# A selective-scan kernel on one core: GpSimd's work taken as pairs of state groups, and a convolution's taps gathered into one part

## The chip, the core and the metric

The kernel runs on one core of a Trainium2 chip. The core has five engines that run their own instruction streams: TensorE (PE in the profile), VectorE (DVE), ScalarE (ACT), GpSimd (POOL) and SyncE (SP), which here issues nearly all DMAs. Each engine takes its instructions strictly in the order in which they stand in its stream; between engines there are semaphores only. SBUF is the on-chip memory of 128 partitions, PSUM the small memory into which TensorE accumulates. The metric is the device time of one execution in microseconds (us).

## What is computed

The input is a batch of 32 images, 96 channels, 56 x 56. Layer 0 is a ConvNeXt block, layer 1 two Mamba blocks with a fusion and a batch norm. Cut to what matters:

```python
# layer 0
h = depthwise_conv7x7(x) + conv_b
h = layernorm_over_channels(h)
x1 = layer_scale * (gelu(h @ w1 + b1) @ w2 + b2) + x
# layer 1: seq is x1 as (batch, 3136 tokens, 96); two times:
h = layernorm(seq)
xs, z = split(h @ in_w)                       # 192 channels each
xc = silu(causal_conv4(xs) + conv_b)
dt, Bm, Cm = split(xc @ xproj_w)              # 6, 16 and 16 columns
delta = softplus(dt @ dt_w + dt_b)
dA = exp(delta[..., None] * A)                # 192 channels x 16 states
dBx = delta[..., None] * Bm * xc[..., None]
hstates = scan over tokens: h[t] = dA[t] * h[t-1] + dBx[t]
y = sum over states of hstates * Cm + Dp * xc
seq = seq + (y * silu(z)) @ out_w
# then: pooled branch, 1x1 fusion, batch norm over everything, + x1
```

All of it is in 32-bit floats.

## The kernel before, in words

Before the main loop the depthwise convolution of the first 12 images is made on TensorE with banded weight matrices, the weights are folded, and the first image's layer-0 block is made. After the main loop there is a short pass for the batch norm and the output.

**Stages.** The main loop has 256 stages: 32 images x 4 chunks of 784 tokens (`CH`) x 2 Mamba layers. Layers alternate, so a stage's successor is another chunk or the other layer. In a batch's first chunk the scan starts from the constant 0, in the others from a kept state (`st`).

**Steps.** The 192 channels x 16 states of a stage are 3072 recurrences, taken as 24 steps (`NSTEP`) of 128 partitions x 784 tokens. A step n has j = n // 4 (six blocks of 32 channels) and g = n % 4 (four groups of 4 states, `NG`). For each step:

- ScalarE makes the factor exp(delta * A) (`exps`, L890), into PSUM for g = 3 and for the two "pooled" blocks j = 2 and 5, otherwise into an SBUF tile `da`;
- the input product u * B is made by VectorE for the four other blocks (`times_b`, L878). For those TensorE has spread u over the partitions into PSUM just before the block (`spread`, L905). For j = 2 and 5 GpSimd makes it (`pooled`, L915) from a copy of u loaded from DRAM (`us`);
- VectorE scans (`scan`, L938) into one of four slots of a ring, slot g;
- GpSimd multiplies the states by C (L942) into a `da` tile;
- TensorE adds the product up over states into `y` (`add_up`, L975), three steps later (`LAG`);
- after each two blocks VectorE multiplies `y` by the gate (`gate`, L956).

So in the steps of a VectorE block, VectorE makes two products in step 0 and two in step 1 of the block, and scans only in steps 2 and 3.

**B and C.** They are broadcast from DRAM to tiles `bc` of one group each, B and C side by side, eight buffers, in steps 10 and 13 of the stage before (`load_bc`, L679).

**Around it.** Every piece of the other work has a place written by hand as a number: 24 steps make a stage, the whole part names the step after whose own instructions it is issued, and the fraction orders pieces within it. `prep` makes the next stage's normalisation, projections, silu, B, C, delta and u (`product` on GpSimd, L712, in two parts, places 16.9 and 25.2, which is step 1 of the stage itself); `post` projects the finished stage back; `block0` makes half a chunk of layer 0; `conv` makes one channel pair of the convolution for five later images in stages 2 to 193. Its taps (L552) are 14: seven over three images (168 columns) at places 7.7 to 10.4 and seven over two images (112 columns) at 18.5 to 22.2, each part with its own store by ScalarE (L565).

**Order.** The loop writes out, for each step n: the exponentials ahead, the state kept, `scan(n)` with its gates and products, after every fourth step the spread for the next one, the add-ups of step n - 3, then the pieces of the step. This is the order on every engine (a manual schedule); nothing is rearranged. PSUM's eight banks are three general tiles (`ps0` to `ps2`), two double ones (`w0`, `w1`) and `y`.

The main lines of the loop, with the diff's place in them:

```python
if n % NG == NG - 1:
    spread(n + 1)
...
if n % NSTEP in LATE:
    add_up(n - LAG - 1)
if n % NSTEP + 1 not in LATE:
    add_up(n - LAG)
```

Of the kernel before, what the change touches and what calls it, by code (L numbers as in the profile page):

```python
# [34 lines left out]
F32 = mybir.dt.float32  # L35
# [9 lines left out]
C = 96  # L45
DIN = 192
# [15 lines left out]
def convnext_mamba_kernel(  # L62
# [211 lines left out]
    for i in range(2):  # L274
        d = {}
        lg, lb = column(ln_g[i], C, f"lg{i}"), column(ln_b[i], C, f"lb{i}")
        wz = const.tile([C + 1, 2 * DIN], F32, name=f"inw{i}", tag=f"inw{i}")
        norm_weights(wz, in_w[i], lg, lb)
        wx = const.tile([C + 1, 4, DIN], F32, name=f"wx{i}", tag=f"wx{i}")
        nc.gpsimd.dma_start(wx, taps[i].partition_broadcast(C + 1))  # L280
        for k in range(4):
            nc.vector.tensor_tensor(wx[:, k, :], wx[:, k, :], wz[:, 0:DIN], ALU.mult)
        d["wx"], d["wz"] = wx, wz[:, DIN : 2 * DIN]
# [60 lines left out]
    with ExitStack() as main:  # L344
# [7 lines left out]
        def work(shape, name, bufs):  # L352

            pool, n = (pre[0], 3) if pre else (wp, bufs)
            return pool.tile(shape, F32, name=name, tag=name, bufs=n)
# [42 lines left out]
        xins = {}  # L398

        def block0(b, c, s):  # L400
# [16 lines left out]
            def load_x():  # L417
                if s == 0:
                    xins[b, c] = work([C, CH], "xin", 1)
                    nc.sync.dma_start(xins[b, c], x[b, :, c * CH : (c + 1) * CH])  # L420
# [36 lines left out]
            def down():  # L457
                v["ps"] = psum(2)
                nc.tensor.matmul(
                    v["ps"][0:C, 0:HC], eye, xins[b, c][:, tok(s)], start=True, stop=False  # L460
# [7 lines left out]
            def residual():  # L468
                xs = xins[b, c][:, tok(s)]
                nc.scalar.activation(  # L470
                    xs, v["ps"][0:C, 0:HC], AF.Identity, bias=b2ls,
                    accum_out=batch_sums[b][:, k : k + 1],
                )
                if s == 1:
                    nc.sync.dma_start(x1_d[b][:, c * CH : (c + 1) * CH], xins.pop((b, c)))
# [6 lines left out]
            def pool():  # L482
                ps = psum(2)
# [4 lines left out]
            def fuse():  # L488
                ps = psum(2)
# [9 lines left out]
            last = [(21.5, total), (29.9, pool), (30.9, fuse)] if k == 2 * NCH - 1 else []  # L499
# [32 lines left out]
        PARTS = (0, (NB + 1) // 2), ((NB + 1) // 2, NB)  # L532

        def conv(g, p):
# [11 lines left out]
            def tap(part, dw):  # L546
                first, last = PARTS[part]

                def piece():
                    if dw == 0:  # L550
                        v["ps"] = psum(2)
                    nc.tensor.matmul(  # L552
                        v["ps"][0:R2, 0 : (last - first) * W], v["band"][:, dw, :],
                        xpad[:, first:last, dw : dw + W], start=(dw == 0), stop=(dw == 6),
# [4 lines left out]
            def store(part):  # L559
                first, last = PARTS[part]  # L560
                n = (last - first) * W

                def piece():
                    t = wp.tile([R2, HC], F32, name="sq", tag="sq", bufs=3)
                    nc.scalar.activation(  # L565
                        t[:, 0:n], v["ps"][0:R2, 0:n], AF.Identity, bias=cb[:, p : p + 1]
                    )
                    nc.sync.dma_start(
                        conv_d[g][p * R2 : (p + 1) * R2, first * W : last * W], t[:, 0:n]
                    )  # L570

                return piece

            at = (7.7, 8.2, 8.6, 9.2, 9.6, 10.2, 10.4), (18.5, 18.6, 19.2, 20.2, 21.2, 21.3, 22.2)
            return [
                (-1, load), (11.05, store(0)), (22.9, store(1)),
                *[(at[part][dw], tap(part, dw)) for part in range(2) for dw in range(7)],
            ]

# [7 lines left out]
        def prep(S):  # L587
# [77 lines left out]
            def dbl_out():  # L665
# [5 lines left out]
                S.bcs = []  # L671

            def load_bc(gs):
                def piece():
                    for g in gs:
                        t = wp.tile([128, 2, CH], F32, name="bc", tag="bc", bufs=8)
                        for k in range(2):
                            src = v["bd"][NS * k + 4 * g : NS * k + 4 * g + 4, :]
                            nc.sync.dma_start(  # L679
                                t[:, k, :], src.unsqueeze(0).broadcast_to([32, 4, CH])  # L680
                            )
                        S.bcs.append(t)

                return piece
# [23 lines left out]
            def product(lo, hi):  # L708
                def piece():
                    if lo == 0:  # L710
                        S.u = wp.tile([128, NQ, HC], F32, name="u", tag="u", bufs=1)
                    nc.gpsimd.tensor_tensor(  # L712
                        S.u[:, lo:hi], v["dl"][:, lo:hi], S.xc[:, lo:hi], ALU.mult
                    )

                return piece
# [43 lines left out]
            elif S is stages[3]:  # L760
# [14 lines left out]
                (max(10.2, t[8] + 1.2), load_bc((0, 1))), (max(13.2, t[8] + 2.2), load_bc((2, 3))),  # L775
                (t[9], dt), (t[10], softplus),
                (max(16.9, t[10] + 1.5), product(0, 2)), (max(18.3, t[10] + 3.1), store_u(0)),
                (25.2, product(2, 3)), (26.3, store_u(1)),
# [68 lines left out]
        ring = wp.tile([128, NG, CH], F32, name="h", tag="h", bufs=1)  # L847
        LAG = 3
        LATE = (4, 12)
# [23 lines left out]
        def product_tile(S, j, g):  # L873
            t = S.da[j, g] = wp.tile([128, CH], F32, name="da", tag="da", bufs=11)
            return t

        def times_b(S, out, g):
            nc.vector.tensor_tensor(  # L878
                halves(out), S.u4.rearrange("p (a b) -> p a b", a=2)[:, :, 0:HC],
                halves(S.bcs[g][:, 0, :]), ALU.mult,  # L880
            )

        def exps(n):
# [5 lines left out]
            e = wide(g % 2)[:, 0:CH] if in_psum(j, g) else product_tile(S, j, g)  # L889
# [248 lines left out]
```

## Time and profile before

| | us |
|---|---|
| three runs | 16960.82, 16963.9 (median), 16972.59 |
| the profiled execution | 16951.94 |
| its span, first to last instruction | 16950.2 |
| first exponentials and scans of the main loop | about 560 |
| last product of the main loop (L942) | 16582.5 |

| engine, 2000 us from 8000 to 10000 | busy us |
|---|---|
| PE | 1885.41 |
| DVE | 1898.28 |
| ACT | 1414.16 |
| POOL | 1951.42 |

In the profile a line such as L942 is a line of the kernel. A group gives engine, operation, output<-inputs with their shapes, the count, busy time and mean length, and then the time for which the engine stood idle before these instructions with what released it. TensorE shows two instructions for each 32-bit matmul, so x4 in one add-up are two matmuls. A timeline gives start, length, engine, line and a count of instructions that followed one another.

### The profile page before, as it was taken

To read this page: it belongs to the slowest core of one execution; us is meant where nothing else is said; L and a number is where in the kernel's file an instruction comes from. 1 tells how busy PE (TensorE), PEld (TensorE's weight loads), DVE (VectorE), ACT (ScalarE), POOL (GpSimd) and SP (SyncE) were. 2 spreads that over 40 slices of the span, in tenths; PEclk is the share of its full clock that TensorE was granted. 3 is DMA by queue.
4 is the path that set the end of the run, shared out by engine and by line. 5 is a ranking of instruction groups with operands and counts; after the bars stand their busy time and mean duration, and the time that the engine had idled before them with its cause. 6 is when DMAs were issued, how large, how long until landed. Compare 5 with 4: busy or idle time off the path is not lost. (4 is left out here: it accounts for less than half of the span.)

```text
span 16950.2 us, 206740 instructions
## 1 busy us (share of the span) xinstructions
PE 15327.0 (90%) x69336; PEld 5507.9 (32%) x69336; DVE 15667.8 (92%) x12351; ACT 11444.5 (68%) x18723; POOL 15657.7 (92%) x8798
## 2 busy tenths in 40 slices
PE   8899999999999999999999999999998888888881
PEld 5333333333333333333333333333332222222220
DVE  8699999999999999999999999999999999999994
ACT  1577777777777777777777777677776777676653
POOL 1699999999999999999999999999999999999991
PEclk9899999999999999999999999999999999999985
DMA  4344444444444444444444444444443433433338
GB/s 113 109 139 142 142 135 140 139 142 141 135 142 140 142 135 140 142 141 137 138 141 141 142 134 141 140 143 137 137 142 131 133 126 129 134 132 133 125 121 280
DMA packets 1303109, 2362.11 MB, mean 139 GB/s; under 512 B 516398, under 2 KB 669242, under 8 KB 1302040
## 3 DMA queue, kind: packets, MB, share of 16 engines
q1 hardware_dynamic: 1292712, 2308.46, 42.0%
q10 hardware_dynamic: 7168, 38.54, 0.6%
q8 instruction: 546, 8.95, 0.2%
q14 instruction: 523, 4.28, 0.1%
q0 software_dynamic: 2160, 1.88, 0.1%
HBM read 1945.97 MB, written 402.41 MB: 139 GB/s over the span
## 5 line engine op out<-in xcount | busy, mean ns | idle before, releaser
L942 POOL TENSOR_TENSOR da<-h,bc 128x784 f32<-128x784 f32 x6144 | 11296.0, 1864 | 428.7 <-DVE h L938 356.3
L975 PE MATMUL y<-da,ssum 128*32 128x392 f32 x24576 | 5193.2, 547 | 232.7 <-POOL da L942 229.1
L890 ACT ACTIVATE w<-d,A 128x784 f32<-128x784 f32 x3072 | 2810.9, 916 | 2442.6 <-DVE h L938 2403.6
L938 DVE TENSOR_TENSOR_SCAN h<-w,st,da 128x784 f32<-128x784 f32 x2304 | 4120.7, 1831 | 267.6 <-ACT w L890 261.5
L938 DVE TENSOR_TENSOR_SCAN h<-da,st,w 128x784 f32<-128x784 f32 x2304 | 4176.3, 1834 | 3.6 <-ACT st L949 3.2
L915 POOL TENSOR_TENSOR da<-us,bc 128x784 f32<-128x784 f32 x2048 | 3811.8, 1861 | 0.0
L878 DVE TENSOR_TENSOR w<-w,bc 128x784 f32<-128x784 f32 x3072 | 2910.6, 978 | 325.6 <-PE w L905 257.4
L890 ACT ACTIVATE da<-d,A 128x784 f32<-128x784 f32 x3072 | 2834.6, 939 | 19.0 <-DMA d<-dd 16.0
L633 PE MATMUL ps<-hn,wx 97*64 97x392 f32 x12288 | 2263.2, 503 | 11.0 <-DVE hn L621 11.0
L975 PEld LDWEIGHTS y<-da,ssum 128*32 128x32 f32 x24576 | 1079.4, 116 | 3366.9 <-issue 2015.7
L905 PE MATMUL w<-u,sel 64*128 64x392 f32 x4096 | 992.4, 560 | 555.8 <-DVE h L938 436.8
L938 DVE TENSOR_TENSOR_SCAN h<-w,da 128x784 f32<-128x784 f32 x768 | 1327.4, 1771 | 125.6 <-ACT w L890 118.0
L938 DVE TENSOR_TENSOR_SCAN h<-da,w 128x784 f32<-128x784 f32 x768 | 1345.4, 1773 | 0.0
L633 PEld LDWEIGHTS ps<-hn,wx 97*64 97x64 f32 x12288 | 797.5, 136 | 1422.4 <-issue 1113.2
L712 POOL TENSOR_TENSOR u<-dl,xc 128x784 f32<-128x784 f32 (+1 forms) x512 | 736.9, 1439 | 471.0 <-ACT dl L698 471.0
L552 PE MATMUL ps<-xpad,band 112*112 112x168 f32 (+1 forms) x5376 | 1086.6, 312 | 0.0
L552 PEld LDWEIGHTS ps<-xpad,band 112*112 112x112 f32 x5376 | 709.8, 175 | 1088.3 <-issue 972.7
L690 PE MATMUL ps<-dbl,dtw 6*64 6x392 f32 x3072 | 728.0, 536 | 310.9 <-ACT dbl L668 310.9
L878 DVE TENSOR_TENSOR da<-w,bc 128x784 f32<-128x784 f32 x1024 | 988.0, 965 | 1.0 <-DMA bc<-bd 1.0
L368 ACT ACT_TABLE_LOAD x759 | 973.8, 1283 | 14.2 <-PEq L1125 0.8
L377 ACT ACTIVATE sq<-ps 96x392 f32<-96x392 f32 x768 | 345.1, 490 | 759.9 <-PE ps L372 343.6
L969 PE MATMUL y<-xc,D 128*128 128x392 f32 x1536 | 790.3, 601 | 32.8 <-DVE z L956 32.8
(152 smaller groups left out, 14579.4 us busy)
## 6 DMA issues: line engine op xcount, KB each, us to landing
bc<-bd SPq DMA_DIRECT2D x2048, 392.0 KB, 6.5
d<-dd SPq DMA_DIRECT2D x1536, 392.0 KB, 3.6
us<-uu SPq DMA_DIRECT2D x512, 392.0 KB, 3.3
dd<-dl SPq DMA_DIRECT2D x512, 294.0 KB, 3.7
band<-band_d SPq DMA_DIRECT2D x192, 343.0 KB, 4.3
uu<-u SPq DMA_DIRECT2D x1024, 49.0 KB, 3.0
cv<-conv_d SPq DMA_DIRECT2D x256, 147.0 KB, 3.4
xin<-in_x SPq DMA_DIRECT2D x128, 294.0 KB, 3.9
```

The source lines that it names most:

```text
L368: nc.scalar.preload_act_table_set("natural_log_exp_and_others")
L552: nc.tensor.matmul(v["ps"][0:R2, 0 : (last - first) * W], v["band"][:, dw, :], xpad[:, first:last, dw : dw + W], start=(dw == 0), stop=(dw ...
L633: nc.tensor.matmul(v["x", q][rows(a), 0:HC], weights[:, k, 64 * q : 64 * q + 64], v["hn"][:, o : o + HC], start=(k == 0), stop=(k == last),)
L712: nc.gpsimd.tensor_tensor(S.u[:, lo:hi], v["dl"][:, lo:hi], S.xc[:, lo:hi], ALU.mult)
L878: nc.vector.tensor_tensor(halves(out), S.u4.rearrange("p (a b) -> p a b", a=2)[:, :, 0:HC], halves(S.bcs[g][:, 0, :]), ALU.mult,)
L890: nc.scalar.activation(e, S.d4[j], AF.Exp, scale=S.d["A"][:, j, g : g + 1])
L905: nc.tensor.matmul(S.u4[:, 512 * a : 512 * a + HC], sel[rows(a), j % 2, :], S.u[rows(a), j // 2, :], start=True, stop=True,)
L915: nc.gpsimd.tensor_tensor(product_tile(S, j, g), S.us[j], S.bcs[g][:, 0, :], ALU.mult)
L938: nc.vector.tensor_tensor_scan(ring[:, g, :], S.e.pop((j, g)), db, 0.0 if c == 0 else d["st"][:, j, g : g + 1], ALU.mult, ALU.add,)
L942: nc.gpsimd.tensor_tensor(da, ring[:, g, :], S.bcs[g][:, 1, :], ALU.mult)
L969: nc.tensor.matmul(S.y[:, 0:HC], S.d["D"][:, q, :], S.xc[:, q, :], start=True, stop=False)
L975: nc.tensor.matmul(S.y[r0 : r0 + 32, 0:HC], ssum, da[:, tok(a)], start=False, stop=(g == NG - 1),)
```

## The change

GpSimd's work and its operands go by pairs of groups, h = g // 2:

- B and C have their own tiles of two groups: `bp` with 3 buffers, `cp` with 4. B of the second pair is loaded at place 18.3, the others at 10.2 and 13.2.
- The ring has six slots by step number; GpSimd's product with C (L942) is one instruction over two steps, after the scan of the odd step; `da` tiles are pairs, six buffers rather than eleven single ones.
- The pooled input products are one instruction for a pair, in steps 1, 5, 13 and 17; u is made by one instruction at place 16.9.
- `add_up` is called for two steps at once, in even steps: step n adds up n - 4 and n - 3. The third gate of a stage is called in `scan` at step 20 (`GATES`) and no longer in `add_up`.
- The convolution of a stage is one part of five images: seven taps of 280 columns at places 5.2 to 10.4 and one store.
- Input and output of layer 0 (`xin`) go by half chunks; the folded input weights keep only the half for z in a lasting tile; two small matmuls of the pooled branch use other PSUM tiles and places.

```diff
-            def load_x():
-                if s == 0:
-                    xins[b, c] = work([C, CH], "xin", 1)
-                    nc.sync.dma_start(xins[b, c], x[b, :, c * CH : (c + 1) * CH])
+                v["xin"] = work([C, HC], "xin", 1)
+                nc.sync.dma_start(v["xin"], x[b, :, k * HC : (k + 1) * HC])
...
-            at = (7.7, 8.2, 8.6, 9.2, 9.6, 10.2, 10.4), (18.5, 18.6, 19.2, 20.2, 21.2, 21.3, 22.2)
+            at = (5.2, 6.2, 7.2, 8.6, 9.2, 9.6, 10.4)
+            return [(-1, load), (11.05, store), *[(at[dw], tap(dw)) for dw in range(7)]]
...
+            def load_bc(k, h):
+                def piece():
+                    name, n = ("bp", 3) if k == 0 else ("cp", 4)
+                    t = S.bc[k, h] = wp.tile([128, 2, CH], F32, name=name, tag=name, bufs=n)
+                    for gg in range(2):
+                        r = NS * k + 8 * h + 4 * gg
+                        nc.sync.dma_start(
+                            t[:, gg, :],
+                            v["bd"][r : r + 4, :].unsqueeze(0).broadcast_to([32, 4, CH]),
+                        )
...
+            def product():
+                S.u = wp.tile([128, NQ, HC], F32, name="u", tag="u", bufs=1)
+                nc.gpsimd.tensor_tensor(S.u, v["dl"], S.xc, ALU.mult)
...
-                (max(16.9, t[10] + 1.5), product(0, 2)), (max(18.3, t[10] + 3.1), store_u(0)),
-                (25.2, product(2, 3)), (26.3, store_u(1)),
+                (max(16.9, t[10] + 1.5), product), (max(18.5, t[10] + 3.1), store_u(0)),
+                (26.3, store_u(1)),
...
-        ring = wp.tile([128, NG, CH], F32, name="h", tag="h", bufs=1)
+        NR = 6
+        ring = wp.tile([128, NR, CH], F32, name="h", tag="h", bufs=1)
         LAG = 3
-        LATE = (4, 12)
+        GATES = (4, 12, 20)
...
-                nc.gpsimd.tensor_tensor(
-                    product_tile(S, j, g), S.us[j], S.bcs[g][:, 0, :], ALU.mult
-                )
+                nc.gpsimd.tensor_tensor(
+                    pair(S, j, h), S.us[j].unsqueeze(1).broadcast_to([128, 2, CH]), S.bc[0, h],
+                    ALU.mult,
+                )
...
-            nc.gpsimd.tensor_tensor(da, ring[:, g, :], S.bcs[g][:, 1, :], ALU.mult)
+            if g % 2 == 1:
+                k = (n - 1) % NR
+                nc.gpsimd.tensor_tensor(da, ring[:, k : k + 2, :], S.bc[1, g // 2], ALU.mult)
...
-                put(m, [(NG * (j - 2) + 2 * g, pooled(m, j, g)) for g in range(NG)])
+                put(m, [(NG * (j - 2) + 4 * h + 1, pooled(m, j, h)) for h in range(2)])
...
-                    if n % NSTEP in LATE:
+                    if (n - LAG) % 2 == 1:
                         add_up(n - LAG - 1)
-                    if n % NSTEP + 1 not in LATE:
                         add_up(n - LAG)
```

## The prediction

> **What bounds the kernel now.** I read the page's busy table first, then its costliest groups, then the waits of the steady part (2000 to 14000 us), and last the timelines of single engines over one stage. The page's chain of waits accounts for only a few per cent of the span, so I left it.
>
> ```profile
> PE 15327.0 (90%) x69336; PEld 5507.9 (32%) x69336; DVE 15667.8 (92%) x12351; ACT 11444.5 (68%) x18723; POOL 15657.7 (92%) x8798
> ...
> L942 POOL TENSOR_TENSOR da<-h,bc 128x784 f32<-128x784 f32 x6144 | 11296.0, 1864 | 428.7 <-DVE h L938 356.3
> L915 POOL TENSOR_TENSOR da<-us,bc 128x784 f32<-128x784 f32 x2048 | 3811.8, 1861 | 0.0
> ```
>
> GpSimd and VectorE are both near full. In the steady window the 4607 products of L942, 24 a stage, make 192 stages in 12,000 us: 62.5 us a stage.
>
> ```profile
> DVE h L938 <- ACT w L890: 290.0, 200, 2.4
> ...
> POOL da L942 <- DVE h L938: 257.3, 375, 2.3
> ...
> DVE w L878 <- PE w L905: 200.5, 244, 1.1
> ```
>
> So VectorE stalls about 1.5 us a stage on an exponential (290/192) and 1.0 on the spread of u (200/192), and GpSimd waits 1.3 for scans. Next, GpSimd's timeline (start, length, name):
>
> ```profile
> 9029.64 1.09 POOL L712 TENSOR_TENSOR u<-dl,xc 128x392 f32<-128x392 f32 x1
> 9030.62 1.91 POOL L942 TENSOR_TENSOR da<-h,bc 128x784 f32<-128x784 f32 x1
> ...
> 9045.10 10.98 POOL L942 TENSOR_TENSOR da<-h,bc 128x784 f32<-128x784 f32 x6
> 9055.97 1.93 POOL L915 TENSOR_TENSOR da<-us,bc 128x784 f32<-128x784 f32 x1
> ```
>
> Six products fill 10.87 us from start to start, 1.81 each; 392 columns take 0.98. That is 2.12 ns a column and 0.15 us an instruction. GpSimd's work is 32 x 1.81 + 1.81 + 0.98 = 60.7 us a stage. VectorE's, by spacings in its timeline: a group whose products it makes itself 10.66 (four products at 0.885, a scan 1.87, three at 1.75), a pooled group 7.05, three gates at 0.46, three norms 1.37: 4 x 10.66 + 2 x 7.05 + 1.38 + 1.37 = 59.5. Neither alone is 62.5. What ties them is this, at a stage's end:
>
> ```profile
> 9076.44 10.99 POOL L942 TENSOR_TENSOR da<-h,bc 128x784 f32<-128x784 f32 x6
> ...
> 9078.91 0.85 PE L975 MATMUL y<-da,ssum 128*32 128x392 f32 x4
> 9079.70 0.45 PE L552 MATMUL ps<-xpad,band 112*112 112x112 f32 x2
> 9080.08 0.93 PE L905 MATMUL w<-u,sel 64*128 64x392 f32 x4
> ...
> 9081.05 0.98 DVE L878 TENSOR_TENSOR w<-w,bc 128x784 f32<-128x784 f32 x1 [0.90 <-PE w L905]
> ```
>
> The six GpSimd products are those of steps 19 to 23 and 0; the first ends at 9078.25. TensorE adds it up (9078.91), does a conv tap, and only then spreads u for step 24, which VectorE needs to go on. TensorE takes its instructions in order, so **VectorE can't enter a group before the product that ended the group before last is made and added up**, 2.80 us after that product's end here.
>
> **The change, part by part.** *Pairs.* A product of two groups has 1568 columns, not shown in the trace: 0.15 + 1568 x 2.12 ns = 3.48 us. Bounds from the rows: no fixed part saved, 2 x 1.81 = 3.62; the fixed part taken from mean durations of the form 784 and 392 of L712 (1850 and 1028 ns: 206 ns an instruction), 3.42. I take 3.48, since spacings are what a chain consists of. The Trainium skill (Perfetto Trace Analysis, GPSIMD Engine Instruction) also says that reported spans of this engine don't compose and that spacings should be used; the rows agree (1864 ns against 1.81 us), and by durations the sum below would be 0.5 us a stage less. Against the change speaks the Trainium skill's GPSIMD Engine Reference (Performance versus the Vector engine): some 2.6 cycles an element at 1.2 GHz, by which 784 columns are an estimated 1.70 us and a merge saves 0.11, a pair being 3.51 and the sum below 0.3 more.
>
> Sixteen products at 3.48 and u as one of 1176 columns (2.64) make 58.3 us of GpSimd work, 2.4 less than before. That gain is only worth something if GpSimd starts as early as before, and it doesn't: a pair waits for its second scan, TensorE adds two steps at once (1.56 us, not 0.78) at even steps, and the spread for steps 12 and 24 stands behind the pairs 6-7 and 18-19. The whole dependence, with VectorE's step 0 at 0 (a chunk after the first; names by steps):
>
> Scan 1 ends at 7.2. Scan 3 is late as now: its exponential follows the silu of z and a table load and comes about 10.3 after step 0 (9.9 to 10.5 in three stages seen), so scan 3 ends at 12.0, the gate at 12.5, scan 5 at 19.7. GpSimd: pair 0-1 from 7.2 to 10.7, the pooled input product queued in step 1 to 14.2, pair 2-3 to 17.6, pair 4-5 must wait for scan 5, 19.7 to 23.2, pooled product 26.7, pair 6-7 at 30.1. Then two add-ups 1.56, the conv tap now put in step 10 (about 0.5), spread until VectorE starts 0.97 (9080.08 to 9081.05), 0.1 of semaphores: step 12 starts at 33.2, where VectorE alone would have been ready at 30.6. Scan 13 ends at 40.4; GpSimd, idle since 37.1, makes pair 12-13 to 43.9, pooled 47.3, pair 14-15 50.8, u 53.4, pair 16-17 (scan 17 at 52.4) 56.9, pooled 60.4, pair 18-19 63.9. Two add-ups, no conv tap there now, and the spread: 2.63. **Step 24 starts at 66.5**; VectorE alone would be there at 63.5. In a batch's first chunk the eight scans on this path are 0.07 shorter (1.68 without a state): 65.9. Mean 66.4.
>
> The same walk for the kernel before (singles at 1.81, 2.80 to the spread) gives 61.8 where 62.5 is measured. So the loss is 66.4 - 62.5 = 3.9 by the measured side and 4.6 by the difference of the two walks; I take 4.2 a stage. Over 255 stages: +1070 us.
>
> *Conv as one part.* Seven taps and a store go from steps 18 to 22 (2.2 us of TensorE between 9073.98 and 9080.08), and seven of 280 columns replace those of 168. A tap of 168 takes 0.47 alone, one of 112 0.38; by that slope 0.66, by the 0.39 of a 392-column add-up matmul less; I take 0.5. Where it was, a stall of 0.9 at step 0 goes, but that is overtaken by the pair behind the spread; the tap in step 10 adds its 0.5 ahead of step 12 (0.66: 40 us in all). ScalarE stores once (rows 0.39 and 0.35 become about 0.47), off the path.
>
> *Queues.* SP: x and x1 go in halves, one load and one store each stage rather than every second one; one conv store less; the same eight B and C loads, two of them moved to step 18, where they wait for VectorE's step 17. Behind them stand the stores and loads of u and delta; u's load waits for the pooled product of step 17 (60.4) and lands 3.3 later (its row), 13 us before it is read. SP has gaps near 9 us (9021 to 9030); should they not cover the extra issue of 0.5 us, it is 0.5 x 255 = 130 us at most. GpSimd's queue gets no DMA. *Buffers.* A scan needs the ring slot of six steps ago: scan 12 the pair 6-7, done at 30.1 and so earlier than the spread. The product tiles come free with the add-ups of steps 12 and 24, hidden behind the pairs made meanwhile; lost cover costs at most one pair, 3.5 us a stage. *Gates* stay where they were in VectorE's order. Setup adds two copies and the first batch finer loads: nothing, next to 560 us of start.
>
> **The sum** is made on the profiled execution, 16,952 us (span 16,950.2), and its 256 stages: 16,952 + 1,070 = 18,022. The median of the runs lies 12 above it: 18,030.
>
> **Rivals.** (1) *Faster, VectorE as the bound.* If GpSimd keeps up, the 58.3 us lie below VectorE's 59.5 plus the 1.5 exponential stall, 61.0 a stage: -1.5 x 255 = -380, 16,580. For it: GpSimd's 2.4 us are real work saved, and TensorE is relieved where VectorE waits now. Against it: from step 12 to step 24 VectorE needs 30.3 us, while the path by GpSimd is 7.2 + 6 pairs + 2.64 + 2.63. It decides only from a pair of 2.97 us down (break-even with 62.5 at about 3.05, nine pairs being on the path), and no row gives less than 3.42. 11%. (2) *Half the stall:* step 12 isn't late, since scan 3's exponential comes in time (-1.4) and pairs cost 3.42 (-0.5): 64.5, +2.0 x 255 = 510, 17,460. The conv taps moved off TensorE ahead of step 0 speak for it; the order of add-ups, projections and silu there, otherwise kept, against. 15%. (3) *The pairs save nothing:* 3.62 each on nine places and u 2.79 add 1.4, and 0.7 for what the walk misses: 68.5, +6.0, 18,480. 10%. (4) *It cancels,* within 34 us (0.2%, about what a measurement of this kernel can tell from no change): 2%.
>
> The forecast itself has 62%, with its own range 17,650 to 18,350. From 17,350 (rival 2 with 0.4 us a stage to spare) to 18,480 (rival 3) the range leaves out some 2 in 10. Slower: 0.62 + 0.15 + 0.10 = 0.87; same 0.02; faster 0.11.
>
> **What would show it.** L942 has 3072 products of about 3.5 us. GpSimd's busy time falls to about 15,000 us, but it idles 8 us a stage, released by scans. VectorE's busy time stays near 15,670, and its wait for the spread (L905) grows from 1 to some 5.5 us a stage, at steps 0 and 12. I am wrong if a pair comes out near 3.0 us, if those waits stay under 1 us a stage, or if TensorE runs a spread ahead of a waiting add-up.

## The result, and the profile after

The changed kernel takes 18,420.25 us (median of 4 runs, 18,416.65 to 18,424.4), the kernel before 16,968.25 (4 runs): a ratio of 1.0856, 95% interval 1.0837 to 1.0875. The profiled execution took 18,424.4 us, 1,472 more than the one profiled before, or 5.77 us for each of 255 stages.

The page of the changed kernel: its busy table, then its costliest groups (busy time, mean ns | idle time before, main releaser). L931 is the product with C, L860 VectorE's own input product; below, L897 is the pooled input product.

```profile
PE 15553.9 (84%) x66648; PEld 5504.5 (30%) x66648; DVE 15727.0 (85%) x12353; ACT 11403.1 (62%) x18531; POOL 15054.2 (82%) x4446
...
L931 POOL TENSOR_TENSOR da<-h,cp 128x1568 f32<-128x1568 f32 x3072 | 10817.9, 3540 | 2501.7 <-DVE h L925 1256.4
L860 DVE TENSOR_TENSOR w<-w,bp 128x784 f32<-128x784 f32 x3072 | 2912.2, 978 | 1428.6 <-PE w L887 1366.4
```

The work is what the diff says. GpSimd is busy 603 us less than before (15,054.2 against 15,657.7), VectorE and ScalarE about as long as before. VectorE's 59 us more are 0.4%. So the loss is idle time of VectorE and GpSimd, and the waits of 2000 to 14000 us name it (engine, line waited for: us in total, times, longest). The 2110 products of L931 in that window are 176 stages of 68.2 us.

```profile
DVE w L860 <- PE w L887: 943.5, 352, 4.5
DVE z L946 <- PE y L965: 266.4, 176, 2.9
...
DVE h L925 <- ACT w L872: 122.0, 212, 1.0
```

VectorE waits 5.4 us a stage for the spread of u (943.5/176; it was 1.0), 1.5 at the gate, and only 0.7 for exponentials (it was 1.5). GpSimd's own waits in that window:

```profile
POOL da L931 <- PE ps L616: 845.3, 174, 5.1
POOL da L931 <- DVE h L925: 813.8, 330, 4.9
```

That is 9.4 us a stage. The first row names a projection on TensorE that the product doesn't read: it came last by the profile's reckoning, and the timeline below shows what GpSimd waited for, the scan of step 1. A stage with a kept state, step 0 at 8011.09; GpSimd:

```profile
8018.48 3.50 POOL L931 TENSOR_TENSOR da<-h,cp 128x1568 f32<-128x1568 f32 x1 [4.93 <-PE ps L616]
...
8030.24 3.51 POOL L931 TENSOR_TENSOR da<-h,cp 128x1568 f32<-128x1568 f32 x1 [1.34 <-DVE h L925]
8033.71 3.56 POOL L897 TENSOR_TENSOR da<-us,bp 128x1568 f32<-128x1568 f32 x1
8037.23 10.62 POOL L931 TENSOR_TENSOR da<-h,cp 128x1568 f32<-128x1568 f32 x3
8051.32 3.50 POOL L931 TENSOR_TENSOR da<-h,cp 128x1568 f32<-128x1568 f32 x1 [3.47 <-DVE h L925]
...
8071.42 10.58 POOL L931 TENSOR_TENSOR da<-h,cp 128x1568 f32<-128x1568 f32 x3
```

These are pair 0-1, which starts as scan 1 ends (8018.3), pair 4-5, the pooled product, pairs 6-7 to 10-11, pair 12-13, and pairs 18-19 to 22-23. VectorE's only stalls on the spread in this stretch, and TensorE at the last of them:

```profile
8043.92 0.98 DVE L860 TENSOR_TENSOR w<-w,bp 128x784 f32<-128x784 f32 x1 [0.95 <-PE w L887]
...
8079.45 0.98 DVE L860 TENSOR_TENSOR w<-w,bp 128x784 f32<-128x784 f32 x1 [4.36 <-PE w L887]
```

```profile
8074.97 2.83 PE L965 MATMUL y<-da,ssum 128*32 128x392 f32 x8 [4.63 <-POOL da L931]
8077.73 1.68 PE L887 MATMUL w<-u,sel 64*128 64x392 f32 x4
```

The predicted chain is there: pair 18-19 is done at 8074.97, TensorE adds up two steps, then spreads, and VectorE goes on at 8079.45. What the prediction didn't have are the lengths. The same eight matmuls of an add-up take 1.51 us elsewhere in the stage, here 2.83, and the spread 1.68 instead of 0.93. The windows of this kernel show the clock that goes with it (start:end, window, busy of PE, PEld, DVE, ACT and POOL, then the granted TensorE clock, DMA share, GB/s):

```profile
8068.00:8070.50 2.50, 2.34 (x12) 0.65 (x10) 2.50 (x2) 0.92 (x1) 2.50 (x1) 1.00 0.86 266
8070.50:8074.90 4.40, 0.00 (x0) 0.00 (x0) 3.80 (x3) 3.95 (x5) 4.40 (x3) 0.85 0.41 139
8075.00:8079.00 4.00, 4.00 (x12) 1.03 (x12) 0.09 (x1) 1.76 (x3) 4.00 (x2) 0.50 0.85 246
```

The granted clock is 1.00 before TensorE goes idle, falls within the idle stretch, and is 0.50 for the add-ups and the spread that VectorE waits for. Ahead of step 12 TensorE idles 1.93 us only, and the add-up takes 1.51:

```profile
8040.85 1.51 PE L965 MATMUL y<-da,ssum 128*32 128x392 f32 x8 [1.93 <-POOL da L931]
```

It is so throughout: between 4000 and 14000 us all 148 double add-ups behind an idle time of 4.3 to 4.7 us took 2.8 us, and all 144 behind one of 1.3 to 2.0 us took 1.5.

### The profile page after: what moved, and what is told of

Its sections match the earlier page's. It is cut to its first block, busy times and chain, and to the rows that moved or that the text cites. A ratio compares the mean times of both kernels' runs of the same rounds, so it can differ in the third digit from the quotient of the medians.

```text
span 18422.7 us, 195286 instructions
## 1 busy us (share of the span) xinstructions
PE 15553.9 (84%) x66648; PEld 5504.5 (30%) x66648; DVE 15727.0 (85%) x12353; ACT 11403.1 (62%) x18531; POOL 15054.2 (82%) x4446
## 4 chain that ended last, share of the span: by engine, by line
POOL 36%; PE 23%; DVE 18%; issue 16%; ACT 3%; DMA 3%; POOLq 0%; SPq 0%; DVEq 0%; ACTq 0%
POOL da L931 24%; DVE h L925 13%; POOL da L897 10%; PE y L965 9%; PE ps L616 6%; DVE w L860 5%; PE w L887 4%; POOL u L694 2%; PE ps L176 2%; ACT w L872 1%; DMA fr<-x_d 1%; ACT L370 1%; PE ps L546 1%; DMA out_y<-fo 1%; ACT z L629 1%
## 5 line engine op out<-in xcount | busy, mean ns | idle before, releaser
L931 POOL TENSOR_TENSOR da<-h,cp 128x1568 f32<-128x1568 f32 x3072 | 10817.9, 3540 | 2501.7 <-DVE h L925 1256.4
L965 PE MATMUL y<-da,ssum 128*32 128x392 f32 x24576 | 5482.6, 574 | 1814.6 <-POOL da L931 1813.4
L860 DVE TENSOR_TENSOR w<-w,bp 128x784 f32<-128x784 f32 x3072 | 2912.2, 978 | 1428.6 <-PE w L887 1366.4
L897 POOL TENSOR_TENSOR da<-us,bp 128x1568 f32<-128x1568 f32 x1024 | 3623.0, 3538 | 0.0
L965 PEld LDWEIGHTS y<-da,ssum 128*32 128x32 f32 x24576 | 1286.0, 120 | 5488.7 <-issue 2766.2
L629 ACT ACTIVATE xc<-ps,cb 128x392 f32<-128x392 f32 x768 | 422.9, 585 | 1677.0 <-PE ps L616 1673.8
L694 POOL TENSOR_TENSOR u<-dl,xc 128x1176 f32<-128x1176 f32 x256 | 686.5, 2682 | 472.0 <-ACT dl L682 472.0
L860 DVE TENSOR_TENSOR da<-w,bp 128x784 f32<-128x784 f32 x1024 | 987.7, 965 | 0.0
L546 PE MATMUL ps<-xpad,band 112*112 112x280 f32 x2688 | 845.4, 429 | 0.7 <-ACT dl L682 0.7
L946 DVE TENSOR_TENSOR z<-y,z 128x392 f32<-128x392 f32 x768 | 423.5, 551 | 443.4 <-PE y L965 442.3
```

The costliest lines, as they stand in the source:

```text
L546: nc.tensor.matmul(v["ps"][0:R2, 0 : NB * W], v["band"][:, dw, :], xpad[:, :, dw : dw + W], start=(dw == 0), stop=(dw == 6),)
L694: nc.gpsimd.tensor_tensor(S.u, v["dl"], S.xc, ALU.mult)
L860: nc.vector.tensor_tensor(halves(out), S.u4.rearrange("p (a b) -> p a b", a=2)[:, :, 0:HC], halves(S.bc[0, g // 2][:, g % 2, :]), ALU.mult,)
L897: nc.gpsimd.tensor_tensor(pair(S, j, h), S.us[j].unsqueeze(1).broadcast_to([128, 2, CH]), S.bc[0, h], ALU.mult,)
L931: nc.gpsimd.tensor_tensor(da, ring[:, k : k + 2, :], S.bc[1, g // 2], ALU.mult)
L965: nc.tensor.matmul(S.y[r0 : r0 + 32, 0:HC], ssum, da[:, tok(a)], start=False, stop=(g == NG - 1),)
```

## The experiments

Twelve kernels were run, each timed beside the kernel before on the same chip, which had medians of 16,951.18 to 16,957.62 us there. Theory A is the prediction's chain (scan, pair, add-ups, spread, VectorE), later with the half clock in it. The three questions were: is it the chain, what does the half clock weigh, and which of the parts costs what.

### Is it the spread behind the add-ups? A lag of four slots

The first of these kernels is the changed kernel with the add-ups one slot later, so that the spread goes ahead of the add-up of pairs 6-7 and 18-19.

```diff
-        LAG = 3
-        GATES = (4, 12, 20)
+        LAG = 4
+        GATES = (5, 13, 21)
```

> The changed kernel with LAG 4 and the gates at steps 5, 13 and 21: the two add-ups of a pair go to odd steps, so that at steps 11 and 23 the spread for the next block stands ahead of the add-ups of the pairs 6-7 and 18-19 in TensorE's order. Nothing else is changed. Theory A (the loss is the chain pair - add-ups - spread): VectorE no longer waits for GpSimd at steps 0 and 12, and the stage falls to VectorE's 59.5 plus the 1.5 of the late exponential, 61.0 us; 16,952 - 1.5 x 255 = 16,570, at most 16,750. Rival B (pairs make GpSimd start late, whatever TensorE's order, and this alone sets the stage): little changes, 18,000 to 18,420. Rival C (six ring slots or six pair tiles bound VectorE next): between, about 17,300.

Measured: 17,368.62 us, ratio 1.0245 (1.0231 to 1.0259). One slot takes back 1,050 of the 1,450 us. So most of the loss is indeed the wait behind the add-ups. But 415 us stay, and theory A's 16,750 at most is missed by 620. Rival C is near in number, but the waits from 4000 to 12000 us (124 stages) don't show its cause: VectorE waits 289 us for exponentials, 157 for the spread and 85 at the gate, but only 33 for anything of GpSimd, and GpSimd 2.6 for an add-up.

The kernel before with the same lag, as a control, first with its gates left where they were:

```diff
-        LAG = 3
+        LAG = 4
...
-                    if n % NSTEP in LATE:
-                        add_up(n - LAG - 1)
-                    if n % NSTEP + 1 not in LATE:
-                        add_up(n - LAG)
+                    add_up(n - LAG)
```

> The kernel before with LAG 4: each step's add-up one step later, so that at steps 11 and 23 the spread stands ahead of the add-up of steps 7 and 19. GpSimd works in single groups as before. Theory A: the same chain costs the kernel before its 0.9 us at step 0; GpSimd's own 60.7 us then set the stage, with the rest of its waits (about 0.5): 61.2 x 256, 16,952 - 1.3 x 255 = 16,620. If pairs are worth anything once the chain is gone, this must be slower than the changed kernel with the same lag by up to GpSimd's 2.4 us a stage less what VectorE takes of it. Rival B: order of spread and add-up does not matter in either kernel: 16,960.

Measured: 17,517.08 us, 1.033 (1.0316 to 1.0344). Both expectations are missed, and it is no control: here a gate now waits for an add-up that comes a slot later (1.7 to 2.1 us at steps 12 and 20 in its timeline). The clean control moves the gates along:

```diff
-        LAG = 3
-        LATE = (4, 12)
+        LAG = 4
+        LATE = (5, 13, 21)
...
-                if j == 4:
-                    gate(n - 1)
```

> The kernel before with each product with C and its add-up two slots later behind the scan (a lag of 4 slots), and the gates moved with them to slots 5, 13 and 21, so that no gate waits for an add-up. Theory A (with the add-up out of the way of the spread, single groups go at the engines' own pace, GpSimd 60.7 us and VectorE 59.5 of 62.5): 62 to 63 us a stage, 16,850 to 17,100; against the changed kernel with the same lag and the old convolution, 17,198, single groups are faster by 100 to 350. Rival (pairs are worth their 2.4 us of GpSimd a stage once the chain is out of the way): 17,200 or more. If it is under 16,900, the lag is worth having by itself.

Measured: 16,960.38 us, 1.0 (0.999 to 1.0009). With single products the lag makes no difference to the time, although it does take the wait at step 0 away (0.1 us a stage on average from 4000 to 12000 us, where it was 0.8). Other waits take its place. In that window VectorE waits 212.6 us for the spread, nearly all of it at step 12 (151.0 before), 149.6 at the gate (23.0 before) and 38.1 for exponentials (197.8 before): 406 us in all, where it was 376. The lag mends the pairs' chain, not the kernel before.

### What does the half clock weigh?

Filler matmuls into a free PSUM tile keep TensorE busy while it would otherwise idle; nothing reads the filler's results. First ten of them in slot 21.9 of the changed kernel:

```diff
+        def filler(m):
+            def piece():
+                ps = psum(2)
+                for k in range(10):
+                    nc.tensor.matmul(
+                        ps[0:32, 0:HC], ssum, stages[m].xc[:, k % NQ, :], start=True, stop=True
+                    )
+
+            return piece
...
+            put(m, [(21.9, filler(m))])
```

> The changed kernel with ten idle matmuls of 392 columns (their result is not used) put on TensorE at step 21, just where it waits 4.6 us for the pair 18-19 in the trace of the changed kernel. There the two add-ups behind the wait took 2.83 us and the spread 1.68, where 1.51 and 0.93 are usual, so 4.55 us pass from the pair's end to VectorE's step 0 and not the 2.63 I had reckoned. Theory A: TensorE runs at half speed after it stood idle; with the wait filled (10 x 0.33 = 3.3 us of the 4.6) the add-ups come back to 1.5 us and the spread to 0.93, 1.9 us a stage x 255: 17,940 us. The Trainium skill (TensorE: Matmul & The Clock Gate, Part 1) says the same, with an idle window of about 3.4 us. Rival B: the add-ups are slow because they read what GpSimd has just written, or for another reason that has nothing to do with idleness; then the filler changes nothing or costs a little: 18,420 to 18,600.

Measured: 18,430.03 us, 1.0868 (1.0853 to 1.0883), no gain. That is rival B's number, but not its reason: the clock stayed at 1.00 and the spread behind the add-ups took 0.93 us, but the filler lasted 5.9 us and made the add-ups start 1.2 us after the pair. The one replaced the other. Six instead of ten:

```diff
-                for k in range(10):
+                for k in range(6):
```

> The filler of the earlier experiment cut from ten matmuls to six. With ten the granted clock stayed at 1.00 over the wait, but the filler took 5.9 us and not 3.3, so the add-ups came 1.2 us after the pair's end, and the time was the same. Six take 12 x 0.316 = 3.8 us of the 4.6. Theory A (half clock after idleness costs 1.9 us at step 0): the add-ups start with the pair's end at full clock, step 0 comes 2.6 us after the pair and not 4.5: 18,420 - 1.9 x 255 = 17,940. Rival B (the half clock is not what delays step 0): 18,420.

Measured: 18,281.39 us, 1.0784 (1.0766 to 1.0802): 140 gained where 480 were expected. TensorE in this kernel, at the end of a stage and at its step 12:

```profile
9004.56 1.51 PE L975 MATMUL y<-da,ssum 128*32 128x392 f32 x8 [0.71 <-POOL da L931]
9006.00 0.93 PE L887 MATMUL w<-u,sel 64*128 64x392 f32 x4
...
9037.34 2.83 PE L975 MATMUL y<-da,ssum 128*32 128x392 f32 x8 [3.27 <-POOL da L931]
```

The end of the stage is as predicted now: step 0 follows at 9006.98, 2.4 us after the add-ups begin. The add-ups read a fresh pair as before and take 1.51, so that isn't what made them slow. But the stage is in another phase against its other work: at step 12 TensorE now idles 3.27 us, where it idled 1.9, and there the add-up is the slow one, at 2.83. On average from 4000 to 12000 us the half from step 12 to step 24 falls from 35.5 to 33.7 us, and the half from step 0 to step 12 grows from 32.8 to 33.8. So both places got filler, four in slot 9.9 and six in slot 21.9:

```diff
-            put(m, [(21.9, filler(m))])
+            put(m, [(9.9, filler(m, 0, 4)), (21.9, filler(m, 2, 6))])
```

> The changed kernel with filler matmuls on TensorE ahead of both places where it otherwise idles before the add-ups: 4 into a free psum tile in slot 9.9 and 6 in slot 21.9. Theory A (the half clock at the end of the chain is all that lies between the predicted 66.5 us a stage and the measured 68.4): both add-ups of a chain's end are at 1.5 us and the spread at 0.93, a stage is 66.4 to 66.8 us, 17,900 to 18,020. Rival (the time only moves on to another wait, as when the fill stood at the second half alone, 18,281): 18,250 or more. Rival (the filler itself delays the add-ups as 10 of them did): 18,400.

Measured: 18,161.43 us, 1.0707 (1.0691 to 1.0723), between the theories: 260 us gained, some 140 short of A's range. VectorE at three entries of a block behind a spread:

```profile
9002.48 0.98 DVE L860 TENSOR_TENSOR w<-w,bp 128x784 f32<-128x784 f32 x1 [2.31 <-PE w L887]
...
9035.86 0.98 DVE L860 TENSOR_TENSOR w<-w,bp 128x784 f32<-128x784 f32 x1 [0.95 <-PE w L887]
...
9069.31 0.98 DVE L860 TENSOR_TENSOR w<-w,bp 128x784 f32<-128x784 f32 x1 [2.36 <-PE w L887]
```

From step 12 to step 0 it takes 33.45 us, where the changed kernel takes 35.53 and the prediction has 33.3. This half is thereby explained by the clock. The first half went from 32.8 to 33.4 in this stage and to 34.5 and 34.8 in others: a part of the gain is given back there. In one of those (step 12 at 8091.78) the filler itself began late, at 8087.36, just as pair 6-7 was done; the add-ups came 1.3 us after it, at 8088.71, and the gate waited 2.6. TensorE came late to the filler because it had run slowly in the first steps of that stage: its granted clock was 0.50 from 8072.70 to 8077.00, behind the matmuls of L674 and with only 0.60 us of idle time ahead of them. All stages go by this. Of 118 between 4000 and 12000 us, 51 have a first half of 34.4 us or more, and in these the mean clock over the 7 us from the start of L674's matmuls is at most 0.66; the other 67 have at most 33.5 us and a clock of 0.75 or more, and their two halves come to 66.6 us on average, against the 66.5 of the walk. So the remainder goes with half clock at another place of the stage. That is read from the trace; no run tried to keep the clock up there.

### Which part costs what?

The new convolution alone, in the kernel before (with the two small matmuls of the pooled branch that had to change their PSUM tile):

```diff
-            at = (7.7, 8.2, 8.6, 9.2, 9.6, 10.2, 10.4), (18.5, 18.6, 19.2, 20.2, 21.2, 21.3, 22.2)
+            at = (5.2, 6.2, 7.2, 8.6, 9.2, 9.6, 10.4)
+            return [(-1, load), (11.05, store), *[(at[dw], tap(dw)) for dw in range(7)]]
```

> The kernel before with only the convolution of the change (seven taps of 280 columns at places 5.2 to 10.4, one store, the two small matmuls of the pooled branch moved); GpSimd works in single groups. Theory A: it frees TensorE of 2.2 us in steps 18 to 22 and takes away the 0.9 us stall at step 0 in the 192 stages with a convolution, but GpSimd's 60.7 us and its waits then set the stage: 0 to 0.9 us a stage less, 16,800 to 16,960. Rival B: the taps now ahead of the spread of step 12 make a new stall there, 0.3 us a stage: 17,010. Either way the conv part isn't what makes the changed kernel 1,450 us slower.

Measured: 17,377.76 us, 1.025 (1.0236 to 1.0264): both theories missed, by 368 us at least. VectorE near step 12 of this kernel:

```profile
9023.72 0.57 DVE L941 TENSOR_TENSOR z<-y,z 128x392 f32<-128x392 f32 x1 [0.93 <-PE y L960]
9025.24 0.98 DVE L863 TENSOR_TENSOR w<-w,bc 128x784 f32<-128x784 f32 x1 [0.95 <-PE w L890]
```

The stall at step 0 is gone as expected. But seven long taps together with the projection of the finished stage put TensorE behind in steps 5 to 12, and gate and spread now wait 1.9 us there; its waits for an exponential rose as well, to 2.4 us a stage (295.9 us over 123.5 stages, 4000 to 12000 us). The other way round, the changed kernel with the old convolution in two parts:

```diff
-            at = (5.2, 6.2, 7.2, 8.6, 9.2, 9.6, 10.4)
+            at = (7.7, 8.2, 8.6, 9.2, 9.6, 10.2, 10.4), (18.5, 18.6, 19.2, 20.2, 21.2, 21.3, 22.2)
```

> The changed kernel with the convolution as before (14 taps in two parts at the old places); pairs as changed. Alone on the kernel before, the new conv cost 425 us, since TensorE's taps and projection then delay step 12. Theory A (in the changed kernel these taps lie in TensorE's wait for the pair and cost nothing but the last one): 18,300 to 18,560, and the two parts of the change do not add up. Rival B (they add): 18,420 - 425 = 18,000. Rival C: taps in steps 20 and 21 shorten TensorE's idle time at the stage's end below what halves the clock: 1.9 us a stage off where there is a conv, 18,420 - 1.9 x 192 = 18,055, and then the clock in those stretches stays at 1.00.

Measured: 18,489.65 us, 1.0905 (1.0889 to 1.0921). In the changed kernel the new convolution is worth 70 us. This is what is left of two larger effects. TensorE in this kernel, ahead of step 0 and of step 12:

```profile
9002.67 1.51 PE L980 MATMUL y<-da,ssum 128*32 128x392 f32 x8 [3.33 <-POOL da L946]
...
9035.55 2.83 PE L980 MATMUL y<-da,ssum 128*32 128x392 f32 x8 [3.13 <-POOL da L946]
```

The old taps in steps 18 to 22 shorten TensorE's idle time there, from 4.6 to 3.3 us, and in this stage the add-ups run at their usual length, as rival C had it. But ahead of step 12 the shorter taps leave it idle for longer, 3.13 us instead of 1.93, and the add-ups are slow there. On average from 4000 to 12000 us the second half of a stage takes 34.4 us instead of 35.5, and the first 34.3 instead of 32.8. So the time fits theory A, but not because the old taps changed nothing.

Then the pairs' two kinds. The changed kernel with the products with C as single groups, each after its own scan:

```diff
-            if g % 2 == 1:
-                k = (n - 1) % NR
-                nc.gpsimd.tensor_tensor(da, ring[:, k : k + 2, :], S.bc[1, g // 2], ALU.mult)
+            nc.gpsimd.tensor_tensor(
+                da[:, g % 2, :], state(n), S.bc[1, g // 2][:, g % 2, :], ALU.mult
+            )
```

> The changed kernel with GpSimd's products with C made singly again, one after each scan; B, u, the tiles, the add-ups by two and the conv stay as changed. It costs GpSimd 0.15 x 12 = 1.7 us a stage more and takes away the wait for the second scan of a pair. Theory A (the pair's wait for its second scan lies on the path from spread to spread): by the same walk step 12 comes 31.7 after step 0 instead of 33.2, the product of step 19 ends 61.2 after step 0 instead of 63.9, and TensorE waits under 3 us, too short for the half clock seen after 4.6 us: 63.8 us a stage, 16,952 + 1.3 x 255 = 17,280, or 65.7 and 17,770 if the clock still falls. Rival B (what costs is adding up by two behind one another, not the pairs): 18,200 to 18,700, as GpSimd only has more to do.

Measured: 17,288.9 us, 1.0197 (1.0181 to 1.0212), where A had 17,280. Undoing this one instruction takes back 1,130 us, although it gives GpSimd 3072 instructions more. The opposite part alone, only the pooled input products as pairs in the kernel before:

```diff
+                t = wp.tile([128, 2, CH], F32, name="dp", tag="dp", bufs=2)
...
-            t = S.da[j, g] = wp.tile([128, CH], F32, name="da", tag="da", bufs=11)
+            t = S.da[j, g] = wp.tile([128, CH], F32, name="da", tag="da", bufs=7)
...
-                put(m, [(NG * (j - 2) + 2 * g, pooled(m, j, g)) for g in range(NG)])
+                put(m, [(NG * (j - 2) + 4 * h + 2, pooled(m, j, h)) for h in range(2)])
```

> The kernel before with only GpSimd's pooled input products as pairs of two groups (slots 2 and 6, 14 and 18); every product with C stays one group, so that no product waits for a second scan. Theory A (the pairs' loss is the wait for the second scan and for what stands behind the product; the fixed cost of an instruction that a merge saves, 0.15 us, is a gain): 4 merges a stage, between nothing and 0.6 us a stage, 16,800 to 16,955. Rival (the pooled pair also holds back the product with C behind it, since GpSimd takes it earlier than its slot is due): 17,000 to 17,300.

Measured: 18,743.43 us, 1.1055 (1.1037 to 1.1074), outside both. The group of VectorE's products that write a `da` tile (4000 to 12000 us) shows what it ran into:

```profile
L878 DVE TENSOR_TENSOR da<-w,bc 128x784 f32<-128x784 f32 x461 | 445.9, 967 | 502.2 <-PE y L978 502.2
```

VectorE waits 4.4 us a stage (502.2/115.3) before it may write a `da` tile, until TensorE has added up the product that still holds it. The eleven tiles are the same memory as before, but split into seven single ones and two pairs they seem no longer to cover each other's peaks. That is a loss of this experiment's own making; about pairs it says nothing. The next two answer that without it. The changed kernel with lag 4 and the old convolution:

```diff
-        LAG = 3
-        GATES = (4, 12, 20)
+        LAG = 4
+        GATES = (5, 13, 21)
...
-            at = (5.2, 6.2, 7.2, 8.6, 9.2, 9.6, 10.4)
+            at = (7.7, 8.2, 8.6, 9.2, 9.6, 10.2, 10.4), (18.5, 18.6, 19.2, 20.2, 21.2, 21.3, 22.2)
```

> Pairs with LAG 4 (spread ahead of the add-ups) and the convolution as before. With LAG 4 and the new conv the time was 17,369; its stages with a conv took 64.4 us, those without 63.3. Theory A: with the spread out of the chain, the conv's taps ahead of step 12 are no longer hidden by a wait, and their old places save what they cost the kernel before, 1.1 to 1.7 us in 192 stages: 17,369 - 210 to 320 = 17,050 to 17,160. That leaves pairs no better than the kernel before, VectorE setting the stage in both. Rival B: the conv's place does not matter here: 17,370.

Measured: 17,198.15 us, 1.0142 (1.0127 to 1.0157), 170 us below the new convolution with this lag and 38 above theory A's range. And the same with the products with C single:

```diff
-            if g % 2 == 1:
-                k = (n - 1) % NR
-                nc.gpsimd.tensor_tensor(da, ring[:, k : k + 2, :], S.bc[1, g // 2], ALU.mult)
+            nc.gpsimd.tensor_tensor(
+                da[:, g % 2, :], state(n), S.bc[1, g // 2][:, g % 2, :], ALU.mult
+            )
```

> The changed kernel with the lag of 4 slots, the gates behind it and the old convolution (17,198), but every product with C one group again, as soon as its scan is done; the pooled input products stay pairs. Theory A (with the spread out of the add-ups' way, what still makes pairs slower than singles, 17,198 against 16,960, is the wait for the second scan): 16,850 to 17,000. Rival (what is left comes from the pooled pair, which holds GpSimd for 3.5 us at a time, or from the rest of the change, and singles with C save nothing): 17,150 to 17,350.

Measured: **16,908.59 us, 0.9978 (0.9968 to 0.9987)**, 10 runs beside 13 of the kernel before at 16,951.18. VectorE's waits from 4000 to 12000 us, first with pairs with C, then without:

```profile
DVE h L940 <- ACT w L887: 180.4, 183, 1.7
DVE z L961 <- PE y L980: 162.7, 125, 1.4
DVE w L875 <- PE w L902: 59.3, 88, 1.6
DVE h L940 <- POOL da L912: 34.6, 112, 0.8
```

```profile
DVE z L961 <- PE y L980: 160.9, 127, 1.4
DVE h L940 <- ACT w L887: 136.2, 154, 1.5
DVE w L875 <- PE w L902: 62.9, 63, 1.6
DVE h L940 <- POOL da L944: 0.8, 3, 0.3
```

So pairs with C still cost 289 us, 1.1 a stage, with the chain out of the way. Of these 0.7 lie in the four rows (437 us over 125.8 stages against 361 over 128.0). GpSimd's waits suggest a further cause, which wasn't tried: in the slower of the two it also waits for the load of a C tile, which a pair needs whole, and in the other this is 0.6 us in all.

```profile
POOL da L946 <- DMA cp<-bd: 104.9, 104, 1.6
```

The last kernel is the only one below the kernel before, by 0.22%. The interval leaves out 1.0 by little. Its steady stages with a convolution take 62.5 us like those before (3071 products with C in 8000 us against 3069), the ones without it 61.7 instead of 62.3 (973 products in 13000 to 15500 us against 963); 62 such stages make some 40 of the 43 us.

Put together, the medians make a table (us):

| GpSimd's products | lag 3, old convolution | lag 3, new convolution | lag 4, old convolution | lag 4, new convolution |
|---|---|---|---|---|
| all single | 16,951 to 16,958 (before) | 17,378 | 16,960 | |
| pooled input as pairs, C single | | 17,289 | 16,909 | |
| all as pairs | 18,490 | 18,420 (the change) | 17,198 | 17,369 |

Down the columns the first step is -89 and -51 us, the second +1,131 and +289. The last two rows are built on the changed kernel, with its smaller edits; the first row on the kernel before. So the second step is the pairs with C alone, but the first is the pooled pairs together with u in one instruction, the add-ups by two and the rest.

## Why the prediction was right, and where it was off

**The mechanism of the change held, the number less well.** Forecast 18,030, measured 18,420: slower, as said. It lies within the stated 17,350 to 18,480, but 70 us above the forecast's own range of 17,650 to 18,350, which had the 62%. The wider range reached that far for rival 3, pairs that save nothing, and its reason didn't come, since a pair took 3.47 us. That the number is inside is luck in this sense. GpSimd is busy 15,054 where 15,000 were named, VectorE 15,727 where 15,670 were, and GpSimd waits 9.4 us a stage where 8 were. Removing the spread's wait takes back 1,050 us, and making only the products with C single takes back 1,130: the second scan of a pair, and the spread that stands behind two add-ups, are the loss.

VectorE's wait for the spread is 5.4 us a stage where some 5.5 were named, but the agreement is partly chance. The walk has 2.6 at step 12 and 3.0 at step 24; measured are 0.95 and 4.4. Ahead of step 12 another 1.5 us are waited at the gate, and at step 24 half clock makes the wait longer.

**What the kernel before waits for** was misread. The prediction says of it that VectorE can't enter a group before a product is made and added up, and shows the add-up at 9078.91 with the product done at 9078.25. Between the two TensorE didn't wait for GpSimd, it was still at the convolution:

```profile
9078.34 0.65 PE L552 MATMUL ps<-xpad,band 112*112 112x112 f32 x4
```

With a lag of four slots the spread no longer stands behind that add-up, and the kernel before still takes 16,960. So this chain isn't what holds it at 62.5 us a stage. GpSimd's own 60.7 us are most of it; where the rest comes from stays open. For the pairs the same order does bind: there TensorE idles 4.6 us until the pair is done.

**The walk, step by step.** Stage with step 0 at 8011.09:

| from VectorE's step 0, us | predicted | measured |
|---|---|---|
| pair 0-1 starts | 7.2 | 7.4 |
| pair 4-5 starts, behind scan 5 | 19.7 | 19.2 |
| pair 6-7 done | 30.1 | 29.8 |
| step 12 starts | 33.2 | 32.8 |
| then, from step 12: pair 12-13 starts | 7.2 | 7.4 |
| pair 16-17 starts | 20.2 | 20.5 |
| pair 18-19 done | 30.7 | 31.05 |
| step 24 starts | 33.3 | 35.5 |

The pair costs what was taken: from one product's start to the next 3.47 us (8030.24 to 8033.71), against 3.48.

**The term that was mis-sized** is the last: "Two add-ups, no conv tap there now, and the spread: 2.63." It measured 4.48 (8074.97 to 8079.45). I had taken durations from rows where TensorE ran at a granted clock of 1.00, without asking in which state it would be after the idle time that my own walk gave it. The 1.85 us between them are more than the 1.5 us a stage by which the whole forecast fell short; the first half ended 0.4 earlier than predicted. With the clock kept up, the second half takes 33.45 us in the stage shown, where 33.3 were predicted, and 33.7 on average. Over the whole kernel filler at both ends brought 260 us of some 470 (1.85 x 255): in 51 of 118 stages the first half grew, and these are the stages with the lowest clock behind L674.

The Trainium skill (TensorE: Matmul & The Clock Gate, Part 1: The HAM clock gate) has the rule: after an idle window of about 3.4 us the engine runs at half clock, and needs as long a busy stretch to get back. The changed kernel agrees with it: 4.63 us idle were followed by 0.50, 1.93 us were not. Below the rule's figure the runs go both ways: with six filler matmuls 3.27 us idle were followed by an add-up of 2.83; with the old convolution 3.13 us were followed by one of 2.83 and 3.33 by one of 1.51. Why isn't known here. The low clock behind L674 (last section) came with no such idle time ahead of it.

**The convolution.** "Where it was, a stall of 0.9 at step 0 goes, but that is overtaken by the pair behind the spread; the tap in step 10 adds its 0.5 ahead of step 12": in the changed kernel the whole part gains 70 us, but as the difference of a second half 1.1 us longer and a first half 1.5 us shorter than with the old one, which the prediction didn't have. And the working looked at one tap ahead of step 12 and not at the load on TensorE in steps 5 to 12; alone the edit costs 420 us. In the changed kernel that likely lies hidden in idle time. Once the wait for the pairs is gone a part of it reappears: with lag 4 the new convolution is 170 us slower than the old.

**The stall on scan 3's exponential** was taken "late as now". All waits for exponentials together fell from 1.5 to 0.7 us a stage, and the first half came out 0.4 shorter than the walk. That the longer wait at step 0 gives ScalarE the time is likely, but wasn't tried.

**The rivals.** VectorE as the bound (16,580): the changed kernel's stages took 68.2 us, not 61.0. Half the stall (17,460): step 12 was late as said, 2.5 us of waits there, split between gate and spread. The pairs save nothing (18,480): nearest in number, but not the cause, since a pair took 3.47. That pairs can be worth something may be right in one form, as pooled input products, whose operands are ready early: kernels with these, single products with C and the smaller edits came 51 and 89 us below those with single products throughout. What the pooled pairs bring by themselves wasn't shown.

## What to carry to other kernels

Merging two instructions saves a fixed part, here 0.15 us, and makes the result of the first wait for the operands of the second; count the wait, and then look at what stands behind the reader on its in-order engine. Merge what has its operands early, and leave single what a chain between engines passes through. When a change makes an engine idle in front of a piece of the critical path, take the durations of that piece from rows after such an idle time, not from its busy rows.

## What the hardware showed

- TensorE's clock fell to half and rose again within a stage, in each of the stages looked at, and the mean over the run hardly tells of it: 0.908 against 0.943.
- It also fell with hardly any idle time. In the changed kernel TensorE had waited 0.51 us and was then busy throughout, first with 12 matmuls of only 6 rows (L674, 8022.70 to 8025.26); right behind them the clock was 0.57 (the windows below). At all 117 such places between 4000 and 12000 us the mean clock over the next 3.5 us was under 0.6:

```profile
8022.70:8025.20 2.50, 2.50 (x13) 1.06 (x13) 2.50 (x4) 2.47 (x4) 2.50 (x1) 1.00 0.64 226
8025.20:8029.00 3.80, 3.80 (x11) 0.85 (x10) 3.77 (x4) 2.82 (x4) 3.70 (x2) 0.57 0.24 52
```

  An add-up in that stretch took 2.83 us. That the few rows are the reason wasn't tried.
- A fill against the clock's fall has to fit the gap: 10 matmuls of 392 columns (5.9 us) cost as much as they gained, 6 gained 140 us.
- TensorE's matmuls don't start strictly in the order of the program. In the kernel with filler at both ends two add-up matmuls start at 9032.79, ahead of fillers at 9032.87 and 9033.20 that were issued before them. A spread ahead of a waiting add-up, which the prediction named as a sign of being wrong, doesn't occur in the stretches shown.
